# Separate plan places for the high and low parts of a split eviction, and the value eviction's two halves in the other order

## The chip, the cores and the metric

The kernel runs on one core of a Trainium2 chip. The metric is the device time of one execution in microseconds (us). Before the change the median of three runs is 5970.94 us (5969.76 to 5976.89). Five engines work side by side: TensorE (PE; its weight loads are shown as PEld), VectorE (DVE), ScalarE (ACT), GpSimd (POOL), and SyncE (SP), which here only issues DMAs.

## The reference

Two layers over an image of 4 batches, 128 channels and 64 x 64 pixels, all in fp32. Cut to what matters:

```python
# layer 0: attention over 4096 tokens, 4 heads of 32, then residual and layer norm
Q, K, V = (split_heads(x_flat @ W + b) for W, b in ((Wq, bq), (Wk, bk), (Wv, bv)))
attn = softmax(einsum('bhnd,bhmd->bhnm', Q, K) * scale)
y = einsum('bhnm,bhmd->bhnd', attn, V) @ Wo + bo + x_flat
x = (y - mean(y)) / sqrt(var(y) + 1e-5) * gamma + beta
# layer 1: three branches, added
spatial = conv3x3(x) + b
xz = u @ in_proj_w.T                       # a Mamba block over the same 4096 tokens
xs = silu(causal_conv1d(xi) + b);  x_dbl = xs @ x_proj_w.T
dt = softplus(x_dbl[..., :8] @ dt_proj_w.T + dt_b);  B, C = x_dbl[..., 8:24], x_dbl[..., 24:]
h = exp(dt * A) * h + dt * B * xs;  ym = ((h @ C) + xs * D) * silu(z) @ out_proj_w.T
spectral = irfft2(W_spectral * rfft2(x))
out = spatial + spectral + ym
```

## The kernel before

**Work units.** The 4096 tokens of a batch are cut into 8 chunks of 512 queries, 32 chunks in all. A chunk has two *halves*, one for each pair of heads: half H = 2 x chunk + pair, H from 0 to 63. A half runs over 32 key tiles of 128. One key tile of one half is a *step* m (0 to 31). A chunk therefore has 64 steps, `SLOT`. In what follows "even half" and "odd half" go by H.

**The fixed part of a step.** The main loop (lines 1107 to 1152) issues, at each step:

- `scores_for_exp` (499): six products into the two-bank PSUM tile `s2`: high and low part of the queries against the keys, then the negated row maximum (line 507). ScalarE takes the exponential of it into `e` (515). `s2` has one buffer, so the next step's products wait for this exponential.
- `scores_for_max` (454): four products into `s1` (466), for the half that comes next, nine steps ahead. VectorE takes the maximum (473). `s1` has one buffer too.
- `times_values` (518): `e` times V, added up in PSUM tile `po` (527).
- at even steps VectorE's `scan_state` (857): one state row of the Mamba scan of an earlier chunk, which reads the PSUM tile `dA`. At odd steps ScalarE's `scan_decay` (840): the exponential that fills `dA`, a single buffer in PSUM, so that it waits for the scan before it. GpSimd multiplies and adds around them (845, 867, 886).

**The last key tile of a half** has `times_values` evict `po` (lines 534 to 538): rows 0 to 32 by ScalarE, rows 64 to 96 by VectorE, both into the tile `oz`. It is issued in the step m = 0 of the next half, behind that step's exponential and maximum. `po` has one buffer, so the new half's first value product waits for both copies.

**The rest is placed by a plan.** Everything else (projections, residual, layer norm, convolution, Mamba inputs, gates) is written as generators. `Plan.step` (125) visits them in the order of their rank and time. A generator asks by `yield` for places: "P" on TensorE, "A" on ScalarE, "D" on VectorE, "B" for one of two PSUM banks. `plan.release(bank, n)` gives a bank back n steps later. In the body of the run an odd step offers two places each of P, D and A. An even step offers one A, and neither P nor D (lines 1146 to 1149). In the lead-in (t < -9) every step offers four of each. After the last half (`plan.late`) a generator that asks for a single P, A or D goes on in the same visit. A generator that asks for two letters together, "DA", moves only where both are free.

**Three evictions are split in a high and a low part**, so that fp32r products lose no accuracy: keys (`project_kv`, 353), queries (`project_q`, 419) and the input of the step size (`scan_bc`, 731). ScalarE writes the high part from PSUM; VectorE computes the low part from the same PSUM tile and from the high part, so it waits for ScalarE. Each asks for "DA". The low part's DMAs to DRAM (371, 372, 433, 434, 747) follow one step later, on SP's queue.

**Other names used.** `convolve` (930) has two passes of 3x3 taps, `pf_c_0` and `pf_c_1`: for each GpSimd makes differences `d` (944 to 949), TensorE takes them (957, 962), ScalarE and VectorE evict to `ym` (971, 977, 981, 982). `gate` (790) makes `z * sigmoid(z)` for two channel halves: product `pz` (796), eviction `zg` (802), three ScalarE passes with one VectorE pass between (`sigmoid`, 635). `scan_dt` (751) is the softplus: `pdt`, then `dt`, `spe`, `u`, `lnw` on ScalarE. `scan_input` (696) has `pi`, `xi`, and four VectorE taps `conv`. `place_q` (436) and `place_k` (393) load what the projections stored.

Of the kernel before, what the change touches and what calls it, by code (L numbers as in the profile page):

```python
# [161 lines left out]
def attention_then_conv_mamba(  # L162
# [17 lines left out]
    nc = tc.nc  # L180
# [156 lines left out]
    used = [slice(j * HS, j * HS + HD + 1) for j in range(2)]  # L337

    plan = Plan(2, {"x": 2, "f": 1})

    def bank_tile(bank, shape, name):
        return psum.tile(shape, F32, tag=f"m{bank}", name=name)


    def load_x(c, tag, bufs):
        t = att.tile([P, L], F32, tag=tag, name=f"{tag}_{c}", bufs=bufs)
        b, i = divmod(c, NCH)
        nc.sync.dma_start(t, x[b, :, i * L : (i + 1) * L])
        return t
# [3 lines left out]
    def project_kv(b, i):  # L353

        nm = f"{b}_{i}"
        yield "x"
        xk = load_x(b * NCH + i, "xk", 2)
        yield ""
        yield ""
        bank = yield "PB"  # L360
        pk = bank_tile(bank, [P, L], f"pk_{nm}")
        nc.tensor.matmul(pk, Wk, xk, start=True, stop=True)
        yield "DA"
        plan.release(bank, 2)
        hi = att.tile([P, L], F32R, tag="khi", name=f"khi_{nm}")
        lo = att.tile([P, L], F32R, tag="klo", name=f"klo_{nm}")
        nc.scalar.activation(hi, pk, AF.Identity, bias=bk)
        nc.vector.scalar_tensor_tensor(lo, pk, bk, hi, ALU.add, ALU.subtract)
        yield ""
        kd[b, i] = dram.tile([PAIRS * 2, 2, HD, L], F32, tag="kd", name=f"kd_{nm}", bufs=NCH + 2)  # L370
        nc.sync.dma_start(kd[b, i][:, 0], hi.bitcast(F32))
        nc.sync.dma_start(kd[b, i][:, 1], lo.bitcast(F32))
        bank = yield "PB"
        pv = bank_tile(bank, [P, TPC, HEADS, HD], f"pv_{nm}")
        for t in range(TPC):
            nc.tensor.matmul(
                pv[:, t].rearrange("p h d -> p (h d)"),
                xk[:, t * P : (t + 1) * P],
                Wv,
                start=True,  # L380
                stop=True,
            )
        plan.places["x"] += 1
        yield "A"
        plan.release(bank)
        vst = att.tile([P, TPC, HEADS, HD + 1], F32, tag="vst", name=f"vst_{nm}", bufs=1)
        nc.gpsimd.memset(vst[:, :, :, HD:], 1.0)
        nc.scalar.activation(vst[:, :, :, :HD], pv, AF.Copy)
        yield ""
        vd[b, i] = dram.tile([P, TPC, HEADS, HD + 1], F32, tag="vd", name=f"vd_{nm}", bufs=NCH + 2)  # L390
        nc.sync.dma_start(vd[b, i], vst)
# [27 lines left out]
    def project_q(c):  # L419

        yield ""
        bank = yield "PB"
        pq = bank_tile(bank, [P, L], f"pq_{c}")
        nc.tensor.matmul(pq, Wq, xqs[c], start=True, stop=True)
        yield "DA"
        plan.release(bank, 2)
        hi = att.tile([P, L], F32R, tag="khi", name=f"qhi_{c}")
        lo = att.tile([P, L], F32R, tag="klo", name=f"qlo_{c}")
        nc.scalar.activation(hi, pq, AF.Identity, bias=bq)
        nc.vector.scalar_tensor_tensor(lo, pq, bq, hi, ALU.add, ALU.subtract)  # L430
        yield ""
        qd[c] = dram.tile([2, HEADS, HD, L], F32, tag="qd", name=f"qd_{c}")
        nc.sync.dma_start(qd[c][0].rearrange("h d l -> (h d) l"), lo.bitcast(F32))
        nc.sync.dma_start(qd[c][1].rearrange("h d l -> (h d) l"), hi.bitcast(F32))
# [62 lines left out]
    es, po, oz = {}, {}, {}  # L497
# [20 lines left out]
    def times_values(H, m):  # L518

        k = H % PAIRS  # L520
        i, t = divmod(m, TPC)
        assert have["V", i] == H // PAIRS // NCH
        if m == 0:
            po[H] = psum.tile([P, L], F32, tag="o", name=f"po_{H}")
        e = es.pop((H, m))
        for j in range(2):
            nc.tensor.matmul(  # L527
                po[H][used[j], :],
                VA[i][:, t, 2 * k + j, :],
                e[:, j, :],  # L530
                start=m == 0,
                stop=m == NT - 1,
            )
        if m == NT - 1:
            p = po.pop(H)
            oz[H] = att.tile([P, L], F32, tag="oz", name=f"oz_{H}", bufs=1)
            nc.scalar.activation(oz[H][used[0], :], p[used[0], :], AF.Identity)
            nc.vector.tensor_copy(oz[H][used[1], :], p[used[1], :])  # L538

    sums, inverse = {}, {}  # L540

# [154 lines left out]
    def scan_input(c, hf):  # L696
# [31 lines left out]
        if len(xss[c]) == NH:  # L728
            plan.now(1, scan_bc(c))

    def scan_bc(c):

        bank = yield "PB"
        rank = 4 * DTR
        pd = bank_tile(bank, [rank + 2 * NS, L], f"pd_{c}")
        for hf in range(NH):
            nc.tensor.matmul(pd, xpw[:, hf, :], xss[c][hf], start=hf == 0, stop=hf == NH - 1)
        yield "DA"
        plan.release(bank, 2)
        xd = loc.tile([rank + 2 * NS, L], F32, tag="xd", name=f"xd_{c}", bufs=1)  # L740
        x4 = loc.tile([rank, L], F32R, tag="dtr", name=f"dtr_{c}", bufs=1)
        nc.scalar.activation(xd[rank:, :], pd[rank:, :], AF.Copy)
        nc.scalar.activation(x4, pd[:rank, :], AF.Copy)
        nc.vector.scalar_tensor_tensor(x4, x4, less_x[:rank], pd[:rank, :], ALU.mult, ALU.add)
        yield ""
        bcds[c] = dram.tile([2 * NS, L], F32, tag="bc_d", name=f"bcd_{c}")
        nc.sync.dma_start(bcds[c], xd[rank:, :])
        for hf in range(NH):
            plan.now(1, scan_dt(c, hf, x4))

    def scan_dt(c, hf, x4):

        bank = yield "PB"
        pdt = bank_tile(bank, [P, L], f"pdt_{c}_{hf}")
        nc.tensor.matmul(pdt, dtw[:, hf * P : (hf + 1) * P], x4, start=True, stop=True)


        yield "A"
        plan.release(bank)
        z = loc.tile([P, L], F32, tag=f"dt{hf}", name=f"dt_{c}_{hf}")  # L760
        nc.scalar.activation(z, pdt, AF.Identity, bias=col("dt_b", hf))
        e = loc.tile([P, L], F32, tag=f"sg{hf}", name=f"spe_{c}_{hf}", bufs=1)
        yield "A"
        nc.scalar.activation(e, z, AF.Abs)
        yield "A"
        nc.scalar.activation(e, e, AF.Exp, scale=-1.0)
        yield "A"
        u = loc.tile([P, L], F32, tag=f"u{hf}", name=f"u_{c}_{hf}")
        w = u
        nc.scalar.activation(w, e, AF.Identity, bias=ones)  # L770
        bank = yield "AB"
        ln = bank_tile(bank, [P, L], f"lnw_{c}_{hf}")
        nc.scalar.activation(ln, w, AF.Ln)
        yield "DA"
        plan.release(bank, 2)
        nc.scalar.activation(w, w, AF.Identity, bias=minus_one)
        nc.vector.scalar_tensor_tensor(z, z, 0.0, ln, ALU.max, ALU.add)
        nc.gpsimd.tensor_tensor(e, w, e, ALU.subtract)
        nc.gpsimd.tensor_tensor(z, z, e, ALU.subtract)
        nc.gpsimd.tensor_tensor(u, z, xss[c][hf], ALU.mult)  # L780
        dts[c][hf] = z
        us[c][hf] = u

        for _ in range(3):
            yield ""
        yield "A"
        nc.scalar.activation(xss[c][hf], xss[c][hf], AF.Copy, scale=col("D", hf))
        scaled.add((c, hf))
# [286 lines left out]
    for b in range(B):  # L1075


        t0 = (b * NCH - 1) * SLOT + 5
        for i in range(NCH):
            plan.at((b - 1) * NCH * SLOT + i * SLOT + 40 if b else 6 - SLOT + i, 0, project_kv(b, i))  # L1080
            for k in range(PAIRS):
                plan.at(t0 + k * NT + i * TPC, 0, place_k(b, k, i))
            plan.at(t0 + NT + 1 + i * TPC, 0, place_v(b, i))
    plan.at(-20, 0, constants_of_attention())
    plan.at(-4, 2, constants_of_the_rest())
    for H in range(HALVES):
        if H % PAIRS == 0:
            plan.at((H - 1) * NT - LEAD - 30, 0, load_q(H // PAIRS))
            plan.at((H - 1) * NT - LEAD - 22, 0, project_q(H // PAIRS))
        plan.at((H - 1) * NT - LEAD - 8, 0, place_q(H))  # L1090
        plan.at(H * NT - LEAD, 0, maxima(H))
        plan.at((H + 1) * NT + 1, 0, normalise(H, (H + 1) * NT + 12))
# [14 lines left out]
    while t < end or not plan.idle():  # L1107
        H, m = divmod(t, NT)
# [5 lines left out]
        H, m = divmod(t - 1, NT)  # L1114
        last = m == NT - 1
        if last and 0 <= H < HALVES:
            times_values(H, m)
# [32 lines left out]
        if not last and 0 <= H < HALVES:  # L1150
            times_values(H, m)
# [77 lines left out]
```

## Time and profile before

| | us |
|---|---|
| median of three runs | 5970.94 |
| the profiled execution | 5976.93 |
| its span, first to last instruction | 5975.1 |
| first exponential starts | 132.9 |
| last exponential (half 63) starts | 5744.9 |
| an even half, H = 20 (1865.9 to 1955.1) | 89.2 |
| an odd half, H = 21 (1955.1 to 2043.4) | 88.3 |
| an even half of the last batch, H = 52 | 88.4 |
| an odd half of the last batch, H = 53 | 86.3 |

A half is measured from the start of its first exponential to that of the next half's. From half 8 on the halves of one parity repeat almost to a tenth of a microsecond. The last batch (from half 48 on) has no key and value projections left to do. The granted TensorE clock is 0.985 over the span and 1.00 in the stretches between half 8 and the last. The timeline view lists one engine's instructions in the order of their start: start, duration, engine, line, operation, the tiles written and read, the count of merged instructions, and in brackets the idle time before with what ended it. The view of waits lists who waited for whom: total, count and longest.

### The profile page before, as it was taken

To read this page: it belongs to the slowest core of one execution; us is meant where nothing else is said; L and a number is where in the kernel's file an instruction comes from. 1 tells how busy PE (TensorE), PEld (TensorE's weight loads), DVE (VectorE), ACT (ScalarE), POOL (GpSimd) and SP (SyncE) were. 2 spreads that over 40 slices of the span, in tenths; PEclk is the share of its full clock that TensorE was granted. 3 is DMA by queue.
4 is the path that set the end of the run, shared out by engine and by line. 5 is a ranking of instruction groups with operands and counts; after the bars stand their busy time and mean duration, and the time that the engine had idled before them with its cause. 6 is when DMAs were issued, how large, how long until landed. Compare 5 with 4: busy or idle time off the path is not lost. (4 is left out here: it accounts for less than half of the span.)

```text
span 5975.1 us, 84571 instructions
## 1 busy us (share of the span) xinstructions
PE 5766.0 (96%) x31318; PEld 2461.1 (41%) x31318; DVE 4343.8 (73%) x4633; ACT 3535.4 (59%) x4762; POOL 4575.5 (77%) x4657
## 2 busy tenths in 40 slices
PE   5999999999999999999999999999999999999976
PEld 2444444444444444444444444444444444444422
DVE  4557777777777777777777777777777777777657
ACT  1455666665666665666666666666566666666653
POOL 0006888888888888888788888887888888888887
PEclk7999999999999999999999999999999999999988
DMA  4012232323332222323433333222433322222232
GB/s 126 25 34 59 68 73 74 74 71 110 82 93 75 74 71 72 77 68 83 109 86 79 78 70 71 78 72 68 110 76 94 70 66 66 66 72 66 68 93 88
DMA packets 423324, 456.50 MB, mean 76 GB/s; under 512 B 203360, under 2 KB 204928, under 8 KB 422912
## 3 DMA queue, kind: packets, MB, share of 16 engines
q1 hardware_dynamic: 418256, 449.23, 29.6%
q8 instruction: 247, 4.05, 0.3%
q10 hardware_dynamic: 4656, 1.87, 0.1%
q14 instruction: 165, 1.35, 0.1%
HBM read 376.21 MB, written 66.32 MB: 74 GB/s over the span
## 5 line engine op out<-in xcount | busy, mean ns | idle before, releaser
L473 DVE TENSOR_REDUCE part<-s 128x2 f32<-128x1024 f32 x2048 | 2498.1, 1221 | 1340.5 <-PE s L466 1340.3
L515 ACT ACTIVATE e<-s 128x1024 f32<-128x1024 f32 x2048 | 2095.6, 1023 | 2117.1 <-PE s L507 2114.8
L527 PE MATMUL po<-e,V 128*33 128x512 f32 x8192 | 2182.5, 605 | 4.0 <-DVE oz L538 0.3
L507 PE MATMUL s<-Q,K 64*128 64x512 f32 x8192 | 1502.4, 444 | 12.7 <-ACT e L515 5.7
L466 PE MATMUL s<-K,Q 64*128 64x512 f32 x8192 | 1327.9, 401 | 57.8 <-DVE part L473 46.0
L867 POOL TENSOR_TENSOR hs<-hs,bc 128x512 f32<-128x512 f32 x948 | 1212.6, 1279 | 155.4 <-DVE hs L857 87.1
L507 PEld LDWEIGHTS s<-Q,K 64*128 64x128 f32 x8192 | 610.4, 185 | 1737.9 <-ACT e L515 1290.3
L845 POOL TENSOR_TENSOR db<-u,bc 128x512 f32<-128x512 f32 x948 | 1216.8, 1284 | 0.0
L886 POOL TENSOR_TENSOR acc<-acc,hs 128x512 f32<-128x512 f32 x894 | 1146.7, 1283 | 70.1
L857 DVE TENSOR_TENSOR_SCAN hs<-dA,state,db 128x512 f32<-128x512 f32 x826 | 1052.8, 1275 | 70.3 <-ACT dA L840 39.9
L466 PEld LDWEIGHTS s<-K,Q 64*128 64x128 f32 x8192 | 751.8, 186 | 330.4 <-DVE part L473 165.4
L507 PE MATMUL s<-MX,sel 64*128 64x512 f32 x4096 | 815.4, 393 | 0.0
L840 ACT ACTIVATE dA<-dt,negA 128x512 f32<-128x512 f32 x1024 | 703.3, 687 | 152.7 <-DVE V L857 85.8
L866 POOL COPY state<-hs 128x1 f32<-128x1 f32 x858 | 160.5, 187 | 654.4 <-DVE hs L857 654.4
L527 PEld LDWEIGHTS po<-e,V 128*33 128x33 f32 x8192 | 305.5, 109 | 846.8 <-issue 807.7
L507 PEld LDWEIGHTS s<-MX,sel 64*128 64x128 f32 x4096 | 391.2, 184 | 93.9
L962 PE MATMUL pf<-d,cw 128*128 128x256 f32 x768 | 199.1, 396 | 7.3 <-POOL d L944 7.3
L571 POOL TENSOR_TENSOR op<-op,rz 128x512 f32<-128x512 f32 x32 | 41.5, 1298 | 177.2 <-DMA rz<-rd 177.2
L962 PEld LDWEIGHTS pf<-d,cw 128*128 128x128 f32 x768 | 141.1, 193 | 73.0 <-issue 47.4
L857 DVE TENSOR_TENSOR_SCAN hs<-dA,zero,db 128x512 f32<-128x512 f32 x128 | 163.1, 1275 | 2.9 <-POOL db L845 2.6
L893 PE MATMUL acc<-V,cst 128*128 128x512 f32 x140 | 96.3, 795 | 61.7 <-POOL V L867 61.3
L725 POOL TENSOR_TENSOR xs<-xs,sg_x 128x512 f32<-128x512 f32 x64 | 82.2, 1285 | 74.5 <-ACT sg_x L649 74.5
(156 smaller groups left out, 3541.8 us busy)
## 6 DMA issues: line engine op xcount, KB each, us to landing
bc<-bcd SPq DMA_DIRECT2D x487, 512.0 KB
Q<-qd SPq DMA_DIRECT2D x256, 128.0 KB
K<-kd SPq DMA_DIRECT2D x64, 256.0 KB
MX<-md SPq DMA_DIRECT2D x1024, 0.5 KB
K<-bcd SPq DMA_DIRECT2D x42, 256.0 KB
vd<-vst SPq DMA_DIRECT2D x32, 264.0 KB
V<-vd SPq DMA_DIRECT2D x32, 264.0 KB
xq<-in_x SPq DMA_DIRECT2D x32, 256.0 KB
```

What stands on the lines that cost most here:

```text
L466: nc.tensor.matmul(sc[:, j, :], QT[H][rows[j], n, t * P : (t + 1) * P], KK[k][m][rows[j], :], start=n == 0, stop=n == 1,)
L473: nc.vector.tensor_reduce(part[H][:, :, t, m], sc, AX.X, ALU.max)
L507: nc.tensor.matmul(s[:, j, :], sel[rows[j], :] if n == 2 else KK[k][i][rows[j], t * P : (t + 1) * P], mov[rows[j], :], start=n == 0, stop= ...
L515: nc.scalar.activation(e, s, AF.Exp)
L527: nc.tensor.matmul(po[H][used[j], :], VA[i][:, t, 2 * k + j, :], e[:, j, :], start=m == 0, stop=m == NT - 1,)
L840: nc.scalar.activation(dA[c, v], dts[c][hf], AF.Exp, scale=negA[:, k : k + 1])
L845: engine.tensor_tensor(db[c, v], us[c][hf], bcs[c, n][0], ALU.mult)
L857: nc.vector.tensor_tensor_scan(hs, dA.pop((c, v)), db.pop((c, v)), state[:, k : k + 1] if c % NCH else zero, ALU.mult, ALU.add,)
L866: nc.gpsimd.tensor_copy(state[:, k : k + 1], hs[:, L - 1 :])
L867: nc.gpsimd.tensor_tensor(hs, hs, bcs[c, n][1], ALU.mult)
L886: nc.gpsimd.tensor_tensor(accs[c, hf], accs[c, hf], hs, ALU.add)
L962: nc.tensor.matmul(pf[:, k], taps[k][:, dx, :], d[:, k, :, dx : dx + W], start=dx == 0 and not outer, stop=q == 5 or dx == 2 and not outer,)
```

## The change

In the three split evictions the one request "DA" becomes two: "A" for the high part, then, in a later visit, "D" for the low part. The bank's release moves to the second. In `times_values` the two evictions of `po` change places.

```diff
@@ project_kv (the same in project_q)
-        yield "DA"
-        plan.release(bank, 2)
+        yield "A"
         hi = att.tile([P, L], F32R, tag="khi", name=f"khi_{nm}")
         lo = att.tile([P, L], F32R, tag="klo", name=f"klo_{nm}")
         nc.scalar.activation(hi, pk, AF.Identity, bias=bk)
+        yield "D"
+        plan.release(bank, 2)
         nc.vector.scalar_tensor_tensor(lo, pk, bk, hi, ALU.add, ALU.subtract)
@@ times_values
             oz[H] = att.tile([P, L], F32, tag="oz", name=f"oz_{H}", bufs=1)
+            nc.vector.tensor_copy(oz[H][used[1], :], p[used[1], :])
             nc.scalar.activation(oz[H][used[0], :], p[used[0], :], AF.Identity)
-            nc.vector.tensor_copy(oz[H][used[1], :], p[used[1], :])
@@ scan_bc
-        yield "DA"
-        plan.release(bank, 2)
+        yield "A"
         xd = loc.tile([rank + 2 * NS, L], F32, tag="xd", name=f"xd_{c}", bufs=1)
         x4 = loc.tile([rank, L], F32R, tag="dtr", name=f"dtr_{c}", bufs=1)
         nc.scalar.activation(xd[rank:, :], pd[rank:, :], AF.Copy)
         nc.scalar.activation(x4, pd[:rank, :], AF.Copy)
+        yield "D"
+        plan.release(bank, 2)
         nc.vector.scalar_tensor_tensor(x4, x4, less_x[:rank], pd[:rank, :], ALU.mult, ALU.add)
```

No operation, shape or tile is added or taken away. Since all generators draw on the same places and on the same two banks, other work than the edited lines moves with them. How the built program's order differs, chunk by chunk, is part of the prediction.

More of the change, by code (lines that the diff above doesn't have):

```diff
@@ L737, in scan_bc @@
             nc.tensor.matmul(pd, xpw[:, hf, :], xss[c][hf], start=hf == 0, stop=hf == NH - 1)
-        yield "DA"
-        plan.release(bank, 2)
+        yield "A"
         xd = loc.tile([rank + 2 * NS, L], F32, tag="xd", name=f"xd_{c}", bufs=1)
@@ L743, in scan_bc @@
         nc.scalar.activation(x4, pd[:rank, :], AF.Copy)
+        yield "D"
+        plan.release(bank, 2)
         nc.vector.scalar_tensor_tensor(x4, x4, less_x[:rank], pd[:rank, :], ALU.mult, ALU.add)
```

## The prediction

> **What bounds the kernel now.** The page's first part names TensorE:
>
> ```profile
> PE 5766.0 (96%) x31318; PEld 2461.1 (41%) x31318; DVE 4343.8 (73%) x4633; ACT 3535.4 (59%) x4762; POOL 4575.5 (77%) x4657
> ```
>
> The chain of waits holds only the last 6 us, so the body must be read by steps, from the starts of the exponentials (L515) in ScalarE's timeline. Undisturbed steps are 2.34 to 2.36 us; I use 2.345. Work that the plan puts into an odd step lengthens it: one product of 512 columns makes 3.40, so it costs 1.055; eight products of 256 columns 4.28 (1.935); `pf` with the 512-column product and four of 256, 4.27 (1.925); four of 256 alone 3.42 (1.075). What a stretch takes beyond these is stall. Four waits of VectorE are what the edits touch:
>
> ```profile
> DVE klo L368 <- ACT khi L367: 48.6, 26, 15.8
> ...
> DVE dtr L744 <- ACT dtr L743: 36.1, 30, 1.2
> ...
> DVE qlo L430 <- ACT qhi L429: 32.6, 29, 18.7
> ...
> DVE oz L538 <- ACT oz L537: 31.3, 64, 4.2
> ```
>
> They are no loss by themselves; where TensorE stalls decides. Steps 0 to 11 of half 20 (1865.88 to 1900.39) take 34.51. Pure are 12 x 2.345 = 28.14, plus `pq` 1.055 and `pf` 1.925 + 1.935: 33.06. Stall: **1.45**. Most of it lies here (VectorE, ScalarE, TensorE):
>
> ```profile
> 1867.85 0.69 DVE L538 COPY oz<-po 33x512 f32<-33x512 f32 x1 [0.39 <-ACT oz L537]
> 1868.58 1.28 DVE L857 TENSOR_TENSOR_SCAN hs<-dA,state,db 128x512 f32<-128x512 f32 x1
> 1869.78 1.20 DVE L473 TENSOR_REDUCE part<-s 128x2 f32<-128x1024 f32 x1
> ```
>
> ```profile
> 1867.22 0.59 ACT L537 ACTIVATE oz<-po 33x512 f32<-33x512 f32 x1 [0.33 <-PE po L527]
> 1867.72 0.36 ACT L971 ACTIVATE ym<-pf 128x256 f32<-128x256 f32 x1
> 1868.12 1.02 ACT L515 ACTIVATE e<-s 128x1024 f32<-128x1024 f32 x1
> 1869.89 0.69 ACT L840 ACTIVATE dA<-dt,negA 128x512 f32<-128x512 f32 x1 [0.74 <-DVE hs L857]
> 1870.53 0.71 ACT L787 ACTIVATE xs<-xs,vec 128x512 f32<-128x512 f32 x1
> 1871.14 0.71 ACT L776 ACTIVATE u<-u,minus_one 128x512 f32<-128x512 f32 x1
> 1871.75 1.00 ACT L515 ACTIVATE e<-s 128x1024 f32<-128x1024 f32 x1
> ```
>
> ```profile
> 1871.03 0.73 PE L466 MATMUL s<-K,Q 64*128 64x512 f32 x4 [0.49 <-DVE part L473]
> 1871.69 1.05 PE L527 MATMUL po<-e,V 128*33 128x512 f32 x4
> 1872.81 0.74 PE L507 MATMUL s<-Q,K 64*128 64x512 f32 x4
> ```
>
> The reader is to see a wait handed on: VectorE's `oz` stands 0.39 behind ScalarE's, the scan and the maximum follow it, the maximum holds `s1` until 1870.98, the scan holds `dA`, and `dA`, `xs` and `u` make step 1 last 3.63 with no placed TensorE work in it to cover that. Steps 0 to 6 of odd half 21 are the second place: 17.58 for 16.42, stall 1.16. There VectorE has seven `conv` and `xs` passes (0.74 to 0.81 each) besides its maxima and scans, and hardly idles.
>
> **Part 1: keys and queries.** The order of the built instructions puts `qhi` from step 5 to 4 and `khi` from 13 to 12, where only the exponential stands on ScalarE; `qlo`, `klo` and their DMAs keep their step, as does the bank's release, since D was given at odd steps before too. Before, step 5 had `dA`, `qhi` and `xs`: 2.72 + 2.14 = 4.86 for 4.69, stall 0.17 (inside the 1.45 above). At 13, `sg_x` falls into `khi`'s place, so three passes remain; such a pair (step 9) costs 2.67 + 2.07 = 4.74. Gain 0.12 in 22 halves.
>
> **Part 2: `scan_bc`.** `xd` and `dtr` go from step 21 to 20: two passes (0.59 each) after an exponential of 1.02 make 2.2, which fits into 2.345. The old step 21 had `pz` to cover it (3.40, no stall), so nothing is gained there. But the A place of step 20 was `sg_z`'s. The gate comes a step later, loses its turn for a bank, and `convolve` takes it: in the built order the first pass `pf_0` moves from steps 25 and 27 to 21 and 23, `pz` from 21 to 29, the two `ym` differences from step 1 to 27, and **the second pass `pf_1` from steps 7 and 9 of the even half to 1, 3 and 5**. Thus in the 21 even halves 8 to 48. In the seven even halves 50 to 62, `pf_1` moves from 5 and 7 to step 31 of the half before and step 1. This move is what I expect the time to come from: 1.9 us of TensorE work now stand in the step that stalled.
>
> **Part 3: `oz`.** VectorE's copy can start behind its maximum, at 1867.49 rather than 1867.85. But in the built order ScalarE's copy now waits for VectorE's. The Trainium skill ("PSUM — Partial Sum Buffer", section "PSUM bank collisions raise a hardware error") says that two engines may use one bank at once in different 32-partition quadrants; rows 0 to 32 and 64 to 96 are such, so neither order would need a wait and the swap would be worth nothing. The row shows a wait: VectorE starts 0.04 after ScalarE's end. I take the row. ScalarE's copy then starts at 1868.20 instead of 1867.22, and all that is queued behind it (eviction or input passes, the exponential, `dA`, and so the scan) comes about 1.0 later.
>
> *Even halves.* New step 0, with this half's durations: VectorE `oz` 1867.49 to 1868.18, scan to 1869.5, maximum from 1869.4 to 1870.6. ScalarE `oz` to 1868.8, `lnw` (0.59) to 1869.3, exponential to 1870.3, `dA`, `xs`, `u` to 1872.1. TensorE after `s1` at 1868.5: `pf_1` for 1.925, the value product 1870.5 to 1871.5, `s2` with its result at 1872.5. All three arrive before TensorE needs them: no stall. Then steps 3 and 5 hold the rest of `pf_1` over two passes each. Steps 0 to 11 cost 28.14 + 1.925 + (1.055 + 0.967, half of 1.935) + 1.075 = 33.16: 1.35 gained. If the cover is gone, the exponential comes at 1872.12 instead of 1871.75: 0.37 lost. Given back: steps 27 and 31 of the odd half before now have three passes and no TensorE work. Half 5, which has this pattern, shows 2.72 + 2.08 and 2.76 then 2.17: 0.11 and 0.24 over, against 0.07 at step 29 and about 0.12 at 31 now. Net 1.35 - 0.15 = **1.2 in 21 halves**.
>
> In half 52, steps 31 (of 51) to 4 take 16.18 for 15.13: 1.05 stall. The moved `pf_1` covers 31 and 1; steps 25 and 29 give back about 0.2. **0.85 in seven halves.**
>
> *Odd halves.* Nothing covers. The exponential of step 1 goes from 1957.87 to 1958.86, so step 2's `s2` starts at 1959.92 instead of 1958.92. But `s1` of step 2 waited for the maximum until 1960.36, and now finds it done (1959.95) and starts at 1960.73: only 0.37 remains. Over the next five steps VectorE's chain made TensorE wait about 0.3 more (the seventh `s2` starts at 1971.64); now TensorE runs through at 2.345 and reaches that point at 1960.73 - 0.81 + 5 x 2.345 = 1971.65, plus 0.1 for a late restart. I take a loss of 0.1 in 30 halves; the ends are 0.37 lost and 0.36 gained (VectorE's full head start). Halves 1 to 4 have little beside the attention: the value product waits for ScalarE's copy, 0.3 each.
>
> **Moved past queues.** On SP only the lead-in and the end differ. In the lead-in each projection takes a step more, loads of `xk` pass the stores of the neighbour, and the first score products no longer stand behind two projections that wait for DMA; what starts earlier meets the last key block's load, so I take 0, from 3 lost to 3 gained. At the end two output transfers go behind two loads: 0 within 2. On POOL the two differences `d` (0.76 each) go into step 28, where 1.9 us are idle now; the gate's product goes four steps back, and is needed at 18.
>
> **Sum.** 21 x 1.2 = 25.2, 22 x 0.12 = 2.6, 7 x 0.85 = 6.0; less 30 x 0.1 = 3.0 and 4 x 0.3 = 1.2: **29.6 us gained**. The profiled execution took 5976.93, its span 5975.1; it would be 5947. It lies 6 us above the median of 5970.94, so for the median: **5941**.
>
> **Rivals.**
> - *The new wait on ScalarE decides (slower).* Place: `oz` of ScalarE behind VectorE's, ahead of the exponential. If the 1.0 at step 2's `s2` stays in all 30 odd halves (30.0) and `pf_1` doesn't cover in the 28 even ones (28 x 0.37 = 10.4, and 1.2 early), less parts 1's 28 x 0.17 + 2.6 = 7.4: +34, **6005**. For it: nothing in odd step 0 covers. Against: that stretch waits for VectorE anyway. With the even halves as forecast it decides from 1.05 lost per odd half.
> - *GpSimd is the bound (no change).* From 1865.9 to 1893.4 POOL is busy 26.95 of 27.5 us. If the even stretch can't become shorter, what stays is 2.6 - 4.2: **5972**. Against: the 1.5 us of `d` leave just this stretch.
> - *The swap helps as well (more).* Odd halves gain 0.36 instead of losing 0.1: 13.8 more, **5927**.
> - That the edit does nothing is excluded by the built order.
>
> **Chances.** Forecast 0.60, more 0.14, no change 0.14, slower 0.12. A change under 0.2% (12 us) can't be told from none here. Faster by more: 0.75; within: 0.13; slower: 0.12. The range runs from below the third rival, 5918 (with 3 + 2 at both ends of the run and better cover), to 5975, just past the second; the first is left out.
>
> **What would show it.** Right: even halves 8 to 48 last about 88.0 instead of 89.2, with step 1 at 4.3; odd ones stay at 88.2 to 88.4; the waits of `klo`, `qlo`, `dtr` vanish, and ScalarE's `oz` waits for VectorE's about 0.9 in each half. Wrong: odd halves longer by over 0.5, a wait of `pf` for `d` at step 1, or even halves unchanged.

## The result and the profile after

| | before | after |
|---|---|---|
| median, us | 5972.07 (5969.76 to 5976.89) | 5922.27 (5920.20 to 5926.09) |
| runs | 4 | 4 |
| profiled execution | 5976.93 | 5923.27 |
| its span | 5975.1 | 5921.5 |

The ratio of the medians is **0.9916, with a 95% interval of 0.9904 to 0.9928**: 49.8 us are gained, where 29.6 were forecast. (The median of before has one run more than ahead of the prediction.) The first line of the page of the kernel after is almost the old one. TensorE is busy 38 us less with the same 31318 products, so some of what this row counts as busy was no work:

```profile
PE 5727.7 (97%) x31318; PEld 2477.8 (42%) x31318; DVE 4348.9 (73%) x4633; ACT 3526.8 (60%) x4762; POOL 4571.6 (77%) x4657
```

The view of waits (total, count, longest), first of the kernel before, with the two lines that the prediction did not show:

```profile
PEld s L466 <- DVE part L473: 165.4, 311, 2.0
...
PE s L466 <- DVE part L473: 46.0, 88, 1.3
```

and of the kernel after, where the lines moved by one to three:

```profile
ACT oz L540 <- DVE oz L539: 85.4, 63, 1.6
...
PEld s L468 <- DVE part L475: 61.9, 87, 2.0
...
DVE klo L369 <- ACT khi L366: 24.1, 5, 15.3
...
DVE qlo L432 <- ACT qhi L429: 18.8, 1, 18.8
...
PE s L468 <- DVE part L475: 17.9, 26, 1.5
```

Of the 30 waits for `dtr` two are left (3.6 us, in the last half and behind it); those for `klo` and `qlo` fall from 55 to 6, all in the lead-in, with nearly the old longest ones. The wait on `oz` has changed sides, 31.3 us of VectorE for 85.4 of ScalarE, and still the kernel is faster. TensorE's wait for the maximum shrinks as well: 224 fewer loads of `s1`'s weights stand behind VectorE. That is not the gain, though. The same line in two kernels of the next section, first swap_only (the new order of the copies alone, no faster than before), then scan_bc_only (no new order, but the whole gain of the even half):

```profile
PEld s L466 <- DVE part L473: 79.5, 123, 2.0
```

```profile
PEld s L466 <- DVE part L473: 124.4, 240, 2.0
```

The count of these waits follows the order of the copies: where VectorE's copy and maximum come early, TensorE waits for the exponential instead (`PE s` behind `ACT e`: 5.7 us in before, 32.9 in swap_only).

Where the 53.65 us between the two profiled spans lie is read from the starts of the exponentials. (The medians differ by less, since the profiled execution of before lies 4.9 us above its median.) The view by windows (length, then busy time and count of PE, PEld, DVE, ACT and POOL, granted TensorE clock, DMA share, GB/s) with borders at the first and the last exponential, for the kernel before:

```profile
0.00:132.88 132.88, 65.48 (x254) 31.16 (x254) 55.39 (x59) 12.26 (x19) 9.78 (x26) 0.72 0.48 142
132.88:5744.85 5611.97, 5555.72 (x30794) 2373.30 (x30796) 4113.93 (x4378) 3438.60 (x4605) 4390.29 (x4467) 1.00 0.30 74
5744.85:5975.14 230.29, 144.80 (x274) 56.60 (x273) 174.51 (x198) 84.58 (x138) 175.39 (x166) 0.78 0.32 96
```

and for the kernel after:

```profile
0.00:125.30 125.30, 65.27 (x254) 33.10 (x254) 55.41 (x59) 11.94 (x20) 9.78 (x26) 0.74 0.50 150
125.30:5701.02 5575.72, 5525.23 (x30793) 2392.45 (x30794) 4118.12 (x4378) 3429.54 (x4604) 4387.30 (x4468) 1.00 0.30 75
5701.02:5921.49 220.47, 137.24 (x274) 52.23 (x274) 175.36 (x198) 85.34 (x140) 174.48 (x165) 0.82 0.34 101
```

Thus the lead-in gives 7.6 us, the body 36.3 and the end 9.8. The forecast had 29.6, all in the body, with 0 for the other two (within 3 and within 2). The same kernel run again, after_again below, has 123.7 us ahead of the first exponential and 223.1 behind the last, so the size of such a stage is good to 2 or 3 us only. Of the body's 36.3 the 21 even halves 8 to 48 give 33.5 and the halves 49 to 62 6.3; the odd halves 9 to 47 lose 2.3, the rest 1.2. One half each:

| us | before | after | forecast |
|---|---|---|---|
| even half, 8 to 48 (median) | 89.24 | 87.64 | about 88.0 |
| odd half, 9 to 47 | 88.32 | 88.52 | 88.2 to 88.4 |
| a last-batch even plus odd half | 174.70 | 173.83 | about 173.9 |

The even half does what the prediction drew, but for where its border falls. Half 20 begins at 1850.23; ScalarE's timeline there:

```profile
1850.23 1.02 ACT L517 ACTIVATE e<-s 128x1024 f32<-128x1024 f32 x1
1852.52 0.59 ACT L540 ACTIVATE oz<-po 33x512 f32<-33x512 f32 x1 [1.27 <-DVE oz L539]
1853.01 0.58 ACT L776 ACTIVATE lnw<-u 128x512 f32<-128x512 f32 x1
1853.53 1.00 ACT L517 ACTIVATE e<-s 128x1024 f32<-128x1024 f32 x1
1854.44 0.68 ACT L843 ACTIVATE dA<-dt,negA 128x512 f32<-128x512 f32 x1
1855.05 0.71 ACT L790 ACTIVATE xs<-xs,vec 128x512 f32<-128x512 f32 x1
1855.66 0.71 ACT L779 ACTIVATE u<-u,minus_one 128x512 f32<-128x512 f32 x1
1856.68 1.03 ACT L517 ACTIVATE e<-s 128x1024 f32<-128x1024 f32 x1 [0.30 <-PE s L509]
```

and TensorE's:

```profile
1852.21 0.62 PE L468 MATMUL s<-K,Q 64*128 64x512 f32 x4
1852.76 1.13 PE L960 MATMUL pf<-hx,g 128*128 128x512 f32 x2
1853.72 1.03 PE L965 MATMUL pf<-d,cw 128*128 128x256 f32 x4
1854.68 1.05 PE L529 MATMUL po<-e,V 128*33 128x512 f32 x4
1855.66 0.73 PE L509 MATMUL s<-Q,K 64*128 64x512 f32 x4
1856.24 0.40 PE L509 MATMUL s<-MX,sel 64*128 64x512 f32 x2
```

ScalarE stands 1.27 us behind VectorE's copy, and nothing comes of it: from 1852.76 TensorE takes the moved `pf`, finds `oz` done at 1854.68, and the last line of ScalarE now shows the exponential waiting for TensorE, 0.30. In before it was TensorE that waited here. The sign "step 1 at 4.3" did not come: steps 0 and 1 last 3.30 and 3.15. With the old order of the copies (split_only) they last 2.31 and 4.14; the later copy only moves the border between the two. Steps 0 to 11 take 32.94 for 34.52 before; the prediction had 33.16.

### The profile page after: what moved, and what is told of

Same layout as the page of the kernel before. It is cut to its first block, busy times and chain, and to the rows that moved or that the text cites. A ratio compares the mean times of both kernels' runs of the same rounds, so it can differ in the third digit from the quotient of the medians.

```text
span 5921.5 us, 84679 instructions
## 1 busy us (share of the span) xinstructions
PE 5727.7 (97%) x31318; PEld 2477.8 (42%) x31318; DVE 4348.9 (73%) x4633; ACT 3526.8 (60%) x4762; POOL 4571.6 (77%) x4657
## 3 DMA queue, kind: packets, MB, share of 16 engines
q14 instruction: 165, 1.35, 0.1%
## 5 line engine op out<-in xcount | busy, mean ns | idle before, releaser
L509 PE MATMUL s<-Q,K 64*128 64x512 f32 x8192 | 1502.5, 444 | 29.6 <-ACT e L517 26.1
L468 PE MATMUL s<-K,Q 64*128 64x512 f32 x8192 | 1307.5, 396 | 27.4 <-DVE part L475 17.9
L468 PEld LDWEIGHTS s<-K,Q 64*128 64x128 f32 x8192 | 768.4, 185 | 247.5 <-DVE part L475 61.9
L727 POOL TENSOR_TENSOR xs<-xs,sg_x 128x512 f32<-128x512 f32 x64 | 81.9, 1279 | 74.8 <-ACT sg_x L651 74.8
```

Source lines behind the costliest of these rows:

```text
L468: nc.tensor.matmul(sc[:, j, :], QT[H][rows[j], n, t * P : (t + 1) * P], KK[k][m][rows[j], :], start=n == 0, stop=n == 1,)
L509: nc.tensor.matmul(s[:, j, :], sel[rows[j], :] if n == 2 else KK[k][i][rows[j], t * P : (t + 1) * P], mov[rows[j], :], start=n == 0, stop= ...
```

## Experiments

In all the diffs "-" and "+" are against the kernel that the text names. Ratios are to the kernel before, run on the same chip. "First exponential", halves and "end" (from the last exponential on) are from the profiled execution.

| kernel | median, us | ratio | first exp. | even 8 to 48 | odd 9 to 47 | end |
|---|---|---|---|---|---|---|
| before | 5972.07 | 1 | 132.88 | 89.24 | 88.32 | 230.29 |
| after | 5922.27 | 0.9916 [0.9904, 0.9928] | 125.30 | 87.64 | 88.52 | 220.47 |
| split_only | 5927.31 | 0.9920 [0.9908, 0.9933] | 126.53 | 87.67 | 88.59 | 222.59 |
| swap_only | 5969.73 | 0.9992 [0.9983, 1.0001] | 131.45 | 89.18 | 88.26 | 227.77 |
| proj_only | 5955.48 | 0.9968 [0.9957, 0.9979] | 124.35 | 88.78 | 88.31 | 228.10 |
| scan_bc_only | 5933.78 | 0.9935 [0.9922, 0.9947] | 132.71 | 87.61 | 88.63 | 224.81 |
| before_cover | 5954.63 | 0.9970 [0.9960, 0.9980] | 131.75 | 88.68 | 87.80 | 222.14 |
| no_cover | 5959.07 | 0.9975 [0.9965, 0.9985] | 124.15 | 89.01 | 88.51 | 223.00 |
| lead_as_before | 5927.17 | 0.9924 [0.9910, 0.9937] | 132.59 | 87.66 | 88.52 | 219.51 |
| act_oz | 5919.14 | 0.9909 [0.9895, 0.9922] | 126.58 | 87.67 | 88.44 | 222.08 |
| after_again | 5924.75 | 0.9919 [0.9906, 0.9933] | 123.70 | 87.67 | 88.53 | 223.12 |
| after_a0 | 5918.56 | 0.9909 [0.9895, 0.9922] | 126.82 | 87.87 | 88.11 | 223.10 |
| split_only_a0 | 5925.81 | 0.9921 [0.9907, 0.9934] | 125.69 | 87.89 | 88.39 | 222.76 |
| act_oz_a0 | 5907.88 | 0.9894 [0.9880, 0.9907] | 124.89 | 87.87 | 87.87 | 221.12 |

### Which part of the change does it

Four kernels hold one part each, or leave one out. **split_only** is the kernel after with the old order of the copies:

```diff
-            nc.vector.tensor_copy(oz[H][used[1], :], p[used[1], :])
             nc.scalar.activation(oz[H][used[0], :], p[used[0], :], AF.Identity)
+            nc.vector.tensor_copy(oz[H][used[1], :], p[used[1], :])
```

> After without the exchange of the two value copies: ScalarE's copy first again, the three splits kept. The built order gives the same TensorE and GpSimd order as after. Theory 1 (the exchange only hands a wait to ScalarE, which the moved convolution covers in even halves and nothing covers in odd ones): even halves 8 to 48 stay at 87.6 us, odd ones fall from 88.5 to 88.3, halves 1 to 4 by 0.25 each; some 7 us faster than after, 5915. Theory 2 (VectorE's head start by the exchange is a good part of the gain): slower than after by 10 or more, 5932 to 5945.

**swap_only** is the kernel before with the new order of the copies and nothing else:

```diff
+            nc.vector.tensor_copy(oz[H][used[1], :], p[used[1], :])
             nc.scalar.activation(oz[H][used[0], :], p[used[0], :], AF.Identity)
-            nc.vector.tensor_copy(oz[H][used[1], :], p[used[1], :])
```

> Before with the exchange of the two value copies and nothing else; the built order is otherwise that of before. Theory 1: in even halves no convolution stands in step 1, so the later exponential costs about 0.37 us there (28 halves), 0.2 in 30 odd halves, 0.25 in halves 1 to 4: 17 us slower than before, 5989; lead-in and end as before. Theory 2 (the head start helps by itself): 10 to 20 us faster than before, 5950 to 5960.

**proj_only** has separate places in `project_kv` and `project_q` alone (against before):

```diff
-        yield "DA"
-        plan.release(bank, 2)
+        yield "A"
...
         nc.scalar.activation(hi, pk, AF.Identity, bias=bk)
+        yield "D"
+        plan.release(bank, 2)
```

> Before with the separate places for keys and queries only. Theory 1: the lead-in is 7.6 us shorter as in after (first exponential at 125.3 instead of 132.9), pairs of steps 5 and 13 give 28 x 0.17 + 22 x 0.12 = 7.4; the end stays: 15 us faster than before, 5957. Theory 2 (lead-in was chance, or belongs to another part): 7 faster at most, 5965.

**scan_bc_only** has them in `scan_bc` alone:

```diff
-        yield "DA"
-        plan.release(bank, 2)
+        yield "A"
...
         nc.scalar.activation(x4, pd[:rank, :], AF.Copy)
+        yield "D"
+        plan.release(bank, 2)
```

> Before with the separate places in the Mamba input (high and low part of the step size's input) only. The built order moves the second convolution pass to step 1 as after does. Theory 1: even halves 8 to 48 fall from 89.2 to about 87.8, last batch 0.8 per chunk; the end is about 10 us shorter as in after, the lead-in as before: 5930. Theory 2 (the gain comes from VectorE's waits for the high parts of all three, in proportion to 48.6 + 32.6 + 36.1): a third of the gain, 5955.

`scan_bc` alone brings the even half to 87.61, all of what the whole change brings there. Its end is 5.5 us shorter than that of before, not the 10 expected. The projections alone give 0.46 in the even half and 8.5 us ahead of the first exponential, and land at 5955. The 0.46 don't add to the cover: scan_bc_only is without them as short as after. The exchange moves the medians of halves 8 to 48 by no more than 0.07, alone (swap_only against before) or on top of the splits (after against split_only). In the last batch it takes 0.36 off an even half alone, and 0.01 on top.

Two of this group are misses. split_only was to be 7 us faster than after, with odd halves at 88.3; they stay at 88.59, and the two kernels can't be told apart (only halves 1 to 4 are 0.23 shorter each, as expected). In swap_only what the forecast had put at 0.37 for an uncovered even half is not there. Its ScalarE, half 20:

```profile
1864.73 1.01 ACT L515 ACTIVATE e<-s 128x1024 f32<-128x1024 f32 x1
1867.11 0.59 ACT L538 ACTIVATE oz<-po 33x512 f32<-33x512 f32 x1 [1.36 <-DVE oz L537]
1867.60 0.36 ACT L971 ACTIVATE ym<-pf 128x256 f32<-128x256 f32 x1
1867.86 1.01 ACT L515 ACTIVATE e<-s 128x1024 f32<-128x1024 f32 x1
1868.77 0.68 ACT L840 ACTIVATE dA<-dt,negA 128x512 f32<-128x512 f32 x1
1869.38 0.72 ACT L787 ACTIVATE xs<-xs,vec 128x512 f32<-128x512 f32 x1
1869.99 0.72 ACT L776 ACTIVATE u<-u,minus_one 128x512 f32<-128x512 f32 x1
1870.61 1.01 ACT L515 ACTIVATE e<-s 128x1024 f32<-128x1024 f32 x1
```

From `oz` to the exponential of step 2 pass 3.50 us, though the six passes from `oz` to `u` add up to 4.08: a pass of 0.72 is followed by the next after 0.61 or 0.62, one of 0.59 after 0.49. So that exponential starts 5.88 after the half's first, where before has 1871.75 - 1865.88 = 5.87. The later copy is made up for: most of it because `dA` no longer waits for the scan (0.74 in before) and starts 0.91 behind the exponential instead of 1.77, the rest between `ym` and the exponential (0.26 instead of 0.40). Steps 0 to 2 of the even half take 7.99 for 8.00; steps 0 to 6 of the odd half 17.60 for 17.58.

### Is it the cover, or something else that moves with it

**before_cover** has none of the edits. It moves the second convolution pass of the kernel before into the stalled steps by its own request and rank:

```diff
-            for _ in range(4):
+            for _ in range(8 if outer else 4):
                 yield ""
             bank = yield "PB"
...
-        plan.at(t0 + SLOT + 30, 3, convolve(c))
+        plan.at(t0 + SLOT + 30, 2.5, convolve(c))
```

> Before, with none of the change's edits: only the convolution is ranked ahead of the gate, and its second pass waits four steps more, so that in chunks of the first three batches this pass stands at steps 1, 3 and 5 of even halves, as in after; in the last batch it stands at 29 and 31 of the odd half. Theory 1 (TensorE work in the step that stalled is the gain): even halves 8 to 48 fall by 1.2 to 1.5 us, 25 to 32 in all; lead-in as before: about 5940, or 5932 if the end is shorter too. Theory 2 (the gain needs the evictions' own places): within 5 us of before.

**no_cover** is the kernel after with that pass held back to where it stood before, steps 7 and 9:

```diff
-            for _ in range(4):
+            for _ in range(10 if outer else 4):
                 yield ""
             bank = yield "PB"
```

> After, with all its edits, but the second convolution pass waits six steps more, so that it stands at steps 7 and 9 as in before (5 and 7 in the last batch). Theory 1: even halves lose the cover and pay the exchange as well: 1.4 + 0.37 us in 21 halves and 1.5 in seven, about 45 us slower than after, 5965 to 5970. Theory 2: within 8 us of after.

In before_cover, in the first three batches, the pass stands at steps 1, 3 and 5 of the even half. The gate's product `pz` comes into step 7 besides, out of the odd half. Without its 1.055, steps 0 to 11 take 33.92 - 1.055 = 32.87, against 34.52 before and 32.94 after: the cover alone gives the whole gain of these steps, with "DA" still in place. (The even half as such falls by 0.56, not by the 1.2 to 1.5 expected, because of this `pz`.) Even and odd halves together fall by 0.56 + 0.52 = 1.08. In the last batch the same rank puts the pass at steps 29 and 31 of the odd half before instead. There an odd half takes 90.09 for 86.30 and an even one 85.88 for 88.40: with the whole pass in front of the stall, halves 48 to 61 lose 11.1 us. That is why the median missed what was expected; the place decides, not the pass as such.

no_cover is the reverse. In halves 20, 21, 52 and 53 its convolution and gate products stand where those of after do, but for this pass. Even halves are back at 89.01, and of 49.8 us 14.6 are left (its own pair: 5973.71 to 5959.07). It keeps the splits, the exchange and the shorter ends. The expectation had more to lose, since it counted 0.37 of the exchange as returning with the stall. Steps 0 to 2 take 8.12 here for 8.00 in before: 0.12 return. That the even half stays 0.23 under before comes from step 7, which is 0.30 shorter, as in proj_only.

### Where the lead-in's time comes from

**lead_as_before** keeps "DA" for the projections in the lead-in alone (against after, the same in `project_q`):

```diff
-        yield "A"
+        lead = plan.t < -LEAD
+        yield "DA" if lead else "A"
...
-        yield "D"
-        plan.release(bank, 2)
+        if not lead:
+            yield "D"
+        plan.release(bank, 2)
```

> After, but in the lead-in the keys' and queries' projections ask for both places together as before. Theory 1: only the lead-in changes; the first exponential comes back to 132.9 us, 7.6 us slower than after, 5930; body and end as in after. Theory 2 (the first exponential's time was chance, or the score products were held by the last key block): same as after, 5922.

The first exponential goes back from 125.30 to 132.59, the body stays. What happens is in TensorE's timeline around 50 us. Before:

```profile
42.68 1.16 PE L376 MATMUL pv<-wat_vo,xk 128*128 128x128 f32 x8 [0.38 <-DVE klo L368]
55.58 4.07 PE L362 MATMUL pk<-xk,wk_t 128*128 128x512 f32 x4 [11.74 <-DMA xk<-in_x]
59.58 2.07 PE L466 MATMUL s<-K,Q 64*128 64x512 f32 x8
```

After:

```profile
44.20 0.74 PE L468 MATMUL s<-K,Q 64*128 64x512 f32 x4
50.28 2.05 PE L362 MATMUL pk<-xk,wk_t 128*128 128x512 f32 x2 [5.35 <-DMA xk<-in_x]
52.25 2.07 PE L468 MATMUL s<-K,Q 64*128 64x512 f32 x8
```

Before, the first score products stood behind two key projections that waited 11.74 us for their input, and the first maximum came at 60.84. After, the first of them stand in front, and it comes at 44.97. A half needs 32 maxima before its first exponential. At 82 us the 8th of them has started in before (81.9), the 13th in after (81.4). From there on both kernels make them one behind another, 1.1 to 1.4 us apart, and the 32nd starts at 110.0 and 103.0. So the lead of five maxima is the 7 us. The same two groups show in all fourteen runs: in the nine that ask for the places separately in the lead-in the first exponential starts at 123.7 to 126.8, in the five others at 131.5 to 132.9. The medians can't show it alone: the ratio of lead_as_before, 0.9924, lies inside the interval of after.

### What holds the odd half

**act_oz** gives both copies of `po` to ScalarE, so that VectorE has none and no wait between the two engines is left (against after):

```diff
-            nc.vector.tensor_copy(oz[H][used[1], :], p[used[1], :])
-            nc.scalar.activation(oz[H][used[0], :], p[used[0], :], AF.Identity)
+            for j in range(2):
+                nc.scalar.activation(oz[H][used[j], :], p[used[j], :], AF.Identity)
```

> After, but ScalarE makes both value copies, one behind the other, and VectorE none. No engine waits for the other; ScalarE has 0.5 us more, VectorE 0.7 less. Theory 1: in odd halves VectorE's chain is 1.1 us earlier and the exponential only about 0.5 later than in before; odd halves fall from 88.5 to about 87.8, even ones stay covered, halves 1 to 4 fall by 0.2: 22 us faster than after, 5900. Theory 2 (ScalarE's later exponential decides): odd halves at 88.6 or more, 5925 or more.

A miss: odd halves 88.44, not 87.8, so what VectorE was spared did not shorten them. Three arrangements of the copies (before's, after's, both on ScalarE) all leave odd steps 0 to 6 at 17.5 to 17.6. In each the three passes of `xi` and `carry`, which the plan places at step 0 of an odd half, stand between ScalarE's copy and the exponential of step 1, which here still came 3.63 after the half's first. The next three kernels take ScalarE's place at step 0 away, so that these passes come a step later. The edit is made to after (**after_a0**), split_only (**split_only_a0**) and act_oz (**act_oz_a0**); **after_again** is the kernel after, run once more on the same chip:

```diff
-            plan.step(t, {"D": 0, "P": 0, "A": 1})
+            plan.step(t, {"D": 0, "P": 0, "A": 1 if t % NT else 0})
```

after_again:

> The changed kernel once more, on the chip of the three runs beside it. By all theories 5922 within 5 us; its profile tells whether the lead-in (125.3 us to the first exponential) and the end (220.5 us after the last) come back as they were.

after_a0:

> After, but at the first step of a half, where the value copies stand, the plan offers no place on ScalarE, so that the input passes xi (and lnw) move from behind the copy to the next step. Theory 1 (in odd halves ScalarE's queue ahead of the exponential took over from VectorE's chain): the exponential of step 1 comes 0.8 us earlier, and steps 0 to 6 of odd halves fall from 17.60 to about 17.1; even halves stay covered: 15 us faster than after. Theory 2 (VectorE's chain alone sets these steps): 17.6 as before, same as after.

split_only_a0:

> The same place taken away, but with ScalarE's value copy first, as in the kernel before. Theory 1: here VectorE's chain (waiting 0.39 us for ScalarE's copy) is the later of the two, so steps 0 to 6 of odd halves stay at 17.4 to 17.6: the exchange is worth 0.3 us per odd half once ScalarE has room. Theory 2: like after_a0.

act_oz_a0:

> The same place taken away, and both value copies made by ScalarE, so that VectorE has neither copy nor wait. Theory 1: the shortest of all; steps 0 to 6 of odd halves at 16.9 to 17.1, 15 to 20 us faster than after, about 5903. Theory 2: no faster than the version with both copies on ScalarE and the place left (5919).

after_again came back at 5924.75, with 1.6 us less ahead of the first exponential and 2.7 more behind the last than after had. after_a0 gained 6.2 us on it rather than 15, with odd steps 0 to 6 at 17.30 rather than 17.1; split_only_a0 came out as the first theory has it, and so did act_oz_a0, at 5908 rather than 5903.

ScalarE in half 21 of the kernel after:

```profile
1937.89 1.02 ACT L517 ACTIVATE e<-s 128x1024 f32<-128x1024 f32 x1 [1.25 <-PE s L509]
1940.32 0.59 ACT L540 ACTIVATE oz<-po 33x512 f32<-33x512 f32 x1 [1.40 <-DMA bc<-bcd]
1940.81 0.19 ACT L706 ACTIVATE xi<-carry 128x3 f32<-128x3 f32 x1
1940.90 0.58 ACT L707 ACTIVATE xi<-pi 128x512 f32<-128x512 f32 x1
1941.52 0.20 ACT L708 ACTIVATE carry<-xi 128x3 f32<-128x3 f32 x1
1941.63 1.01 ACT L517 ACTIVATE e<-s 128x1024 f32<-128x1024 f32 x1
```

and of act_oz_a0:

```profile
1931.49 1.02 ACT L517 ACTIVATE e<-s 128x1024 f32<-128x1024 f32 x1 [1.26 <-PE s L509]
1932.93 1.21 ACT L540 ACTIVATE oz<-po 33x512 f32<-33x512 f32 x2 [0.41 <-PE po L529]
1934.16 1.02 ACT L517 ACTIVATE e<-s 128x1024 f32<-128x1024 f32 x1
```

The exponential of step 1 comes 3.74 after the first in the one and 2.67 in the other. Odd steps 0 to 6:

| us | with the place | without |
|---|---|---|
| old order of the copies | 17.59 | 17.57 |
| new order | 17.60 | 17.30 |
| both on ScalarE | 17.49 | 17.05 |

Two limits stand side by side, and each hides the other. TensorE's rows of half 21 name them, first in split_only_a0, then in after:

```profile
1943.10 0.73 PE L468 MATMUL s<-K,Q 64*128 64x512 f32 x4 [0.48 <-DVE part L475]
```

```profile
1942.68 0.73 PE L509 MATMUL s<-Q,K 64*128 64x512 f32 x4 [0.67 <-ACT e L517]
```

In the old order VectorE's late copy and maximum hold the stretch, and the place makes no difference. In the new order VectorE is early, but the exponential is late, until the place goes (TensorE's wait for it in steps 0 to 6 falls from 0.67 to 0.24 in after_a0, the mean of halves 9 to 47). Then VectorE's head start is worth 0.27, close to the 0.36 that the third rival had put there, and 0.52 if it copies nothing at all. (In the 1940.32 row the trace names a DMA as what ended the wait. VectorE's copy, which ended at 1940.28, is what the program has there.)

act_oz_a0 is the fastest kernel of this study: 5907.88 (5906.66 to 5916.39), 16.9 us under the kernel after on the same chip (5922.88 to 5927.86), though its even halves give 0.2 back.

## Why the prediction was right, and where its sizes were off

**What bounds the kernel, and the move of `pf_1`: right, and shown.** The direction and the cause hold: scan_bc_only has the gain, before_cover makes it without any of the edits, no_cover takes it away. Last batch: 0.87 per chunk for 0.85. Halves 1 to 4 lose 0.25 each, for 0.3. But of the 20 us that came beyond the forecast most lie in the lead-in and the end, which had been put at 0. That the total still fell within the range is luck in that part.

**"1.35 gained" in the even half: mis-sized.** It measured 1.60. Steps 0 to 11 gave 1.58. Step 3 was 4.26, as summed; steps 0 and 1 together took 6.45 where 2 x 2.345 + 1.925 = 6.62 had been put, and there lies most of the 0.22 between 33.16 and 32.94. Why these two are shorter than the sum is open.

**"Net 1.35 - 0.15" and a loss of 0.1 in the odd half: right in total, wrong in kind.** Odd halves take 0.20 more. But split_only has 0.27 without the exchange. The loss is in steps 21 to 26 (+0.22) and 27 to 31 (+0.10), which the moved products have left uncovered, with 0.1 regained in steps 7 to 12. The whole pair of halves gained 1.40 for a forecast of 1.2 + 0.12 - 0.1. (VectorE has six `conv` and `xs` passes in steps 0 to 6 of half 21, not seven; nothing hangs on it.)

**"ScalarE's copy waits, all behind it about 1.0 later; if the cover is gone, 0.37 lost": the wait was right, its price wrong.** The copy comes 2.38 after the first exponential in swap_only and 1.34 in before, so 1.04 later. Its wait is 85.4 / 63 = 1.36 us a half, not "about 0.9": the forecast counted only what was added, not the 0.33 that ScalarE had waited for the product before. The forecast had 3.92 from the copy to the exponential of step 2 (1868.20 to 1872.12), swap_only 3.50. 1872.12 is, but for the rounding, the end of the chain drawn for the new step 0 ("to 1872.1"), which has `lnw` where the old order has the shorter `ym`. By the starts in the rows, `lnw` costs 0.52 (half 20 of after) and `ym` 0.26. The forecast also takes `u` to its end, where the next pass starts about 0.1 earlier. The Trainium skill says that ScalarE's activations issued back to back overlap by about 93 ns ("ScalarE: Activation LUTs", section "What ACT_TABLE_LOAD costs"); the rows of swap_only agree with 0.10 to 0.11, and have 0.07 behind `dA`. In no_cover, which has `lnw` there and no cover, 0.12 was lost. For odd halves the reading "s1 waited for the maximum anyway" was right: no more than 0.07 either way. That a wait stands at all between the two copies, where the Trainium skill ("PSUM — Partial Sum Buffer", section "PSUM bank collisions raise a hardware error") lets two engines use different quadrants of one bank at once, was rightly taken from the row: it stands in the new order too. The two copies share `po` and also `oz`; for which of the two tiles the program orders them, no run tells.

**Key pair, "0.12 in 22 halves": too large.** proj_only has 0.05 at odd steps 13 and 14. Its query part gives 0.46 in the even half: 0.17 in steps 5 and 6, as read, and 0.29 in step 7 (4.27 for 4.56), which the reading of the stall had not named.

**"In the lead-in ... I take 0, from 3 lost to 3 gained": failed.** It gained 7.6. The step named both effects (each projection a step longer; the score products no longer behind two projections that wait for DMA), and then let the last key block's load cap them. The load was itself issued earlier, at 92.5 instead of 95.7, and was no cap: the first maximum of that block starts at 99.6, 1.1 behind the one before it, as all do there.

**"At the end ... 0 within 2": failed.** It gained 9.8. Only output transfers were looked at. In the waits of the kernel before stand these lines:

```profile
PE pf L962 <- POOL d L944: 7.3, 1, 7.3
...
DVE ym L977 <- PE pf L962: 9.9, 2, 6.8
```

In before, three chunks still need their second convolution pass when the last exponential starts. The first of these passes waited 7.3 us for its difference, which stood behind the softplus on GpSimd. In the runs where the first line stands (before, swap_only, proj_only) the end takes 227.8 to 230.3; in the eleven others, none of which has it, 219.5 to 224.8. It is not the whole, however. Counted from the last exponential, VectorE's ninth scan starts at 35.0 us in before and 31.0 in after, the 25th at 92.8 and 90.1, the 33rd at 122.7 and 114.2, the last at 218.5 and 208.6. So some 4 us come where that wait is, and most of the rest between 90 and 123 us, where VectorE in before waits 6.8 us for the next chunk's `pf` (in after no `ym` waits longer than 3.1 us for it). But before_cover has such a wait of 7.0 us too, and its end takes 222.1. Neither wait was tried by itself, and the cause of the end's gain is open.

**Rivals.** The first (a slower kernel through ScalarE's wait) falls with swap_only. (Its threshold is 1.09 per odd half by the prediction's own terms, 32.6 / 30, rather than 1.05.) The second (GpSimd the bound) falls with the even half. The third (the swap helps) is wrong for this kernel, yet right once the other limit is gone.

## What to carry to other kernels

In a planned schedule, look first at which stall a moved piece of work lands on: one place asked for differently moved a convolution pass into the stalled step, and that, not the vanished waits, was the gain. Don't take a wait that shrinks for the gain: swap_only lost most of TensorE's waits for the maximum and was no faster. Read the lead-in and the end as stages of their own with their own queues, for a third of the gain came from there. Price a chain on one engine by the distances between starts in the trace, not by the sum of its durations, and with the passes that will really stand in it. Test a step's two limits together, since removing either alone can show nothing.

## What was not expected of the hardware

ScalarE's passes start closer than they last: 0.61 for 0.72, 0.49 for 0.59, 0.91 for 1.01. And TensorE's granted clock is low in the two stages in which it has gaps: 0.78 in the end of the kernel before (TensorE busy 63%) and 0.82 in that of the kernel after (62%), 0.72 and 0.74 in the lead-in (49% and 52%), 1.00 between (99%). Some of what is gained at both ends may be products running at the higher clock; no run tells that apart from the order.
